# A graph layer's edge sums: ring by edge type, bias counts moved ahead, one-hot buffers of four slots, 544 dense chunks in place of 512

## The chip, the cores and the metric

The kernel runs on one core of one Trainium2 chip. The metric is the device time of one execution in microseconds (us). The engines are TensorE (PE, with its weight loads shown apart as PEld), VectorE (DVE), ScalarE (ACT), GpSimd (POOL) and SyncE (SP, which issues plain DMAs).

## The reference, cut to what matters

There are 12500 nodes with 128 features, 200000 edges sorted by their target `dst`, and four edge types with a 128 x 128 weight and a bias each. Targets are drawn as 12500 u^2, so low-numbered nodes have many edges and high-numbered ones few.

```python
h = jnp.maximum(_layernorm(x, axis=-1), 0.0)
xs = h[src]
msgs = zeros
for i in range(4):
    msgs = msgs + jnp.where((edge_types == i)[:, None], xs @ W[i] + b[i], 0.0)
out = x + jax.ops.segment_sum(msgs, dst, num_segments=12500)
```

## The kernel before, in words

**Table.** First, h is computed for all nodes, split into three bf16 parts and written to a table in device memory (htab). The 200000 edges are 1563 chunks of 128. Two methods share them.

**Dense method, first C0 = 512 chunks.** Their edges end in the lowest nodes, which have many edges each. The kernel counts, for every such target, how many edges come from each source and type, and multiplies the counts by the table. `make_slots` first packs the edges into slots of up to 128 edges of one target (or of two neighbouring targets, past node PAIRS = 558). `count` (L928-986) builds for every slot two one-hot matrices on VectorE, o1 (128x128, L943 or L947) and o2 (128x392, L948), makes them up to AHEAD = 8 slots ahead in two pools of 12 buffers, and multiplies them on TensorE (L959); ScalarE writes the counts as bytes (L962). `multiply` (L988-1030) takes a batch of up to VBMAX = 104 targets: for each of the 98 blocks of the table and each of the 3 parts, one matmul with 4 x 104 = 416 columns (L999), 294 per batch; blocks come in as `hs`, four to a buffer (HB = 4). Then four fp32 matmuls with the type weights (L1015) give the result, which is added to `acc`. While one batch is multiplied the next is counted. With C0 = 512 the kernel's own formulas give ND = 1392 targets, 1167 slots, and 14 batches, one of 76 and 13 of 104.

**Gathered method, the other 1051 chunks.** The first 48 take raw rows of x while the table is still being made (`add_up_raw`). For the other 1003, POOL fetches the 128 table rows of a chunk with one indirect DMA (`gather`, L538), ahead of use in a pool of 20 buffers of two chunks. A chunk's targets fall in a window of `win` nodes, 10 at the start and 26 at the end. VectorE makes a one-hot over type and place in the window (L555, 4 x win wide). Groups are of G = 16 chunks, with four short ones (12, 8, 4, 3) at the end, 68 in all. `sum_up` (L563) adds the rows by type and place with three bf16 matmuls a chunk (L572) into a bank `ps` of four chunks, and ScalarE copies it to `sb` (L575). `weigh` (L580) then counts edges by type with four small matmuls on the one-hots (L590), ScalarE casts them (L594), one matmul adds the biases (L597), and four fp32 matmuls with the type weights (L599, each two instructions on the chip) give `py`, 16 x win columns each. VectorE adds each chunk's window into a `ring` of 2048 + 32 nodes, one row of 128 features to a partition (`ring_adds`, L660).

**Leaving.** When no further edge can reach four blocks of 128 nodes (OT = 4), `put_out` sends them: `leave` transposes them (L685), VectorE adds x (L690), SP writes them out (L692), and the ring's stretch is cleared (L707). The dense nodes leave from `acc` in the same way, after the dense work is done.

**Order.** TensorE, VectorE and ScalarE run in the written order of the main loop over groups (from L1268). A group has 8 parts of two chunks. At each part, the loop runs the dense work up to a share set by `pace` (L1038), which spreads the dense columns evenly over the groups and has all of them done at the first part of the last full group; then the bias counts and weights of the previous group (`finish`), that group's ring additions and the next group's one-hots (`side`), evenly over the parts. SP and POOL are ordered by the scheduler of the compiler.

Of the kernel before, what the change touches and what calls it, by code (L numbers as in the profile page):

```python
# [28 lines left out]

# [19 lines left out]
P = 128  # L49
EPS = 1e-5  # L50
UN = 3
G = 16
# [3 lines left out]
C0 = 512  # L56
VBMAX = 104
MANY = 16
HB = 4
AHEAD = 8  # L60
BEHIND = 0.06
RING = 2048
OT = 4
# [3 lines left out]
SOON = (RAW * 16) + HG  # L67

# [4 lines left out]
def kernel(  # L73
# [148 lines left out]
    ring = const.tile([P, RING + WIN], F32, name="ring")  # L222
# [7 lines left out]
    hpool = mid.enter_context(tc.tile_pool(name="rows", bufs=20))  # L230
# [3 lines left out]
    s_ps = mid.enter_context(tc.tile_pool(name="s_ps", bufs=2, space=PSUM))  # L234
    y_ps = mid.enter_context(tc.tile_pool(name="y_ps", bufs=1, space=PSUM))
# [28 lines left out]
    def prep_edges(m0, m1, prep, QB):  # L264
# [15 lines left out]
        pg = x_ps.tile([P, QB, P], F32, name="pt")  # L280
# [12 lines left out]
        pk = x_ps.tile([P, QB, P], F32, name="pt")  # L293
# [178 lines left out]
    banks = [(s_ps, "ps"), (s_ps, "ps"), (y_ps, "py"), (a_ps, "pa")]  # L472
# [87 lines left out]
    finish = []  # L560
    flushing = []

    def sum_up(t0, g, rows, oh, last):  # L563
        win = window_of(C0 + t0)
        K = NT * win
        sb = spool.tile([P, G * KM], F32, name="sb")[:, : G * K].rearrange("p (g t n) -> p g t n", g=G, t=NT)
        for i0 in range(0, g, SG):
            i1 = min(i0 + SG, g)
            ps = s_ps.tile([P, 512], F32, name="ps")[:, : SG * K].rearrange("p (i n) -> p i n", i=SG)
            for i in range(i0, i1):  # L570
                for c in range(3):
                    nc.tensor.matmul(ps[:, i - i0, :], rows(i, c), oh[:, i, :], start=(c == 0), stop=(c == 2))  # L572
                if i % HG and i + 1 < i1:
                    yield (i + 1) / g
            nc.scalar.copy(sb[:, i0:i1].rearrange("p g t n -> p g (t n)"), ps[:, : i1 - i0, :])  # L575
            yield i1 / g

        finish.append(weigh(t0, g, oh, sb, last))

    def weigh(t0, g, oh, sb, last):  # L580
        win = window_of(C0 + t0)

        def bank():
            to = x_ps.tile([P, G * WIN], F32, name="pt") if last else y_ps.tile([P, G * WIN], F32, name="py")
            return to[:, : G * win].rearrange("p (g n) -> p g n", g=G)

        ohv = oh.rearrange("p g (t n) -> p g t n", t=NT)
        pc = bank()
# [6 lines left out]
        yield True  # L595
        py = bank()
        nc.tensor.matmul(py[:, :g, :], b128, cnt[:, :g, :], start=True, stop=False)  # L597
        for t in range(NT):
            nc.tensor.matmul(py[:, :g, :], wsb[:, t, :], sb[:, :g, t, :], start=False, stop=(t == NT - 1))  # L599
        adds.extend(ring_adds(t0, g, lambda i: py[:, i, :], win))  # L600
        yield True


    def add_up_raw(t0, g, rows, marked):
# [20 lines left out]
        sb = spool.tile([P, G * KM], F32, name="sb")[:, : G * K].rearrange("p (g t n) -> p g t n", g=G, t=NT)  # L625
# [19 lines left out]
    def ring_adds(t0, g, of, win):  # L645
        at = []

        def add(i):
# [10 lines left out]
            to = ring[:, bass.ds(at[i], win)]  # L659
            nc.vector.tensor_tensor(to, to, of(i), ALU.add)  # L660
# [16 lines left out]
    def leave(j0, j1, of, c0):  # L677
# [4 lines left out]
        for j in range(j0, j1):  # L682
            r = rows_of(j)
            k = c0 + (j - j0) * P
            nc.tensor.transpose(pt[:r, j - j0, :], of[:, k : k + r], ident)  # L685
# [11 lines left out]

    def put_out(j0, j1, again):

        c0 = j0 * P % RING  # L700
        n = (j1 - j0) * P
        rest = leave(j0, j1, ring, c0) if j0 else lambda: nc.vector.tensor_tensor(acc, acc, ring[:, :n], ALU.add)

        def end():
            rest()
            if again:
                nc.vector.memset(ring[:, c0 : c0 + n], 0.0)  # L707
            if c0 + n == RING:

                nc.vector.tensor_tensor(ring[:, :WIN], ring[:, :WIN], ring[:, RING:], ALU.add)  # L710
                if again:
                    nc.vector.memset(ring[:, RING:], 0.0)

        return end

    flushes = [(0, NDT, 0)]
# [4 lines left out]
    assert NDT * P <= RING - 512  # L721

    def due(jb):
# [11 lines left out]
    goes = [  # L735
        next((i for i in [*range(RAW + 2, FULL), final - 1] if starts[i] + sizes[i] >= c), final)
        for ja, _, c in flushes
    ]
# [4 lines left out]
    def check_chunks():  # L743
# [3 lines left out]
        nc.vector.memset(low, 0.0)  # L747
# [181 lines left out]
    def count(vs, counts):  # L929
# [6 lines left out]
        made = {}  # L936

        def make(k):
            i, s, by, first, last = todo[k]
            o1 = op1.tile([P, P], BF16, name="o1")  # L940
            o2 = op2.tile([P, NB], BF16, name="o2")
            if by == 1.0:
                nc.vector.tensor_scalar(o1, iota_b, loT[:, s : s + 1], None, ALU.is_equal)  # L943
            else:
                if by is None:
                    by = byT[:, (s - PAIRS) // 2 : (s - PAIRS) // 2 + 1]
                nc.vector.tensor_scalar(o1, iota_b, loT[:, s : s + 1], by, ALU.is_equal, ALU.mult)  # L947
            nc.vector.tensor_scalar(o2, iota_n, hkT[:, s : s + 1], None, ALU.is_equal)  # L948
            made[k] = o1, o2

        done = 0
        for k, (i, s, by, first, last) in enumerate(todo):
            while done < min(k + 1 + AHEAD, len(todo)):
                make(done)
                done += 1
            o1, o2 = made.pop(k)
            if first:
                pb = x_ps.tile([P, NB], F32, name="pt")
            nc.tensor.matmul(pb, o1, o2, start=first, stop=last)  # L959
            if last:  # L960

                nc.scalar.activation(  # L962
                    counts[:, :, i * NT : (i + 1) * NT],
                    pb.rearrange("p (b t) -> p b t", t=NT),
                    AF.Copy,
                    accum_out=both[:, i : i + 1],
                )
            yield (k + 1) / len(todo)
        def check_sums():
            n = len(vs) // 2  # L970
            bi = sdp.tile([P, VB // 2], I32, name="bi")
            nc.vector.tensor_copy(bi[:, :n], both[:, :n])
            bb = sdp.tile([P, 2, VB // 2], I32, name="bb")
            nc.vector.tensor_single_scalar(bb[:, 0, :n], bi[:, :n], 255, op=ALU.bitwise_and)
            nc.vector.tensor_single_scalar(bb[:, 1, :n], bi[:, :n], 8, op=ALU.arith_shift_right)
            bf = sdp.tile([P, 2, VB // 2], F32, name="bf")
            nc.vector.tensor_copy(bf[:, :, :n], bb[:, :, :n])
            top = sdp.tile([P, 2], F32, name="top")
            nc.vector.tensor_reduce(top[:, 0:1], bf[:, :, :n], AX.XY, ALU.max)
            nc.vector.tensor_reduce(top[:, 1:2], bf[:, :, :n], AX.XY, ALU.add)  # L980
            nc.vector.tensor_max(most, most, top[:, 0:1])
            nc.vector.tensor_add(held, held, top[:, 1:2])

        tails.append(check_sums)

    tails = []

# [45 lines left out]
    def columns(gi):  # L1033

        K = NT * window_of(C0 + starts[gi])
        return sizes[gi] * (3 * max(64, K) + 5 * K)
# [188 lines left out]
    for g in groups:  # L1225
# [10 lines left out]
    op1 = counting.enter_context(tc.tile_pool(name="op1", bufs=AHEAD + 4))  # L1236
    op2 = counting.enter_context(tc.tile_pool(name="op2", bufs=AHEAD + 4))
    hsp = counting.enter_context(tc.tile_pool(name="hsp", bufs=4))
    raw_sums = outp.tile([P, OT, D], F32, name="xo").rearrange("p j d -> p (j d)")[:, : RAW * G * win_raw]
    nc.scalar.copy(raw_sums, raw_py[:, : RAW * G * win_raw])  # L1240
    raw_adds = [
        ring_adds(m * G, G, lambda i, m=m: raw_sums[:, (m * G + i) * win_raw : (m * G + i + 1) * win_raw], win_raw)
# [8 lines left out]
    ending = []  # L1251
    leaving = []
    soon = []
    rows = gather(RAW * G, G)
    oh, made = one_hots_of(RAW * G, G)
    for m in made:
        m()
    ordered = ExitStack()
    ordered.enter_context(tc.manual_schedule(engines={mybir.EngineType.PE, DVE, mybir.EngineType.Activation}))
    assert min(goes) >= RAW  # L1260
    for gi, (t0, g) in list(enumerate(zip(starts, sizes)))[RAW:]:
# [3 lines left out]
        side = [lambda of=of: ending.append(put_out(*of)) for of in soon]  # L1265
        if gi > RAW and raw_adds:
            side += raw_adds.pop(0)
        soon = list(flushing)  # L1268
        flushing.clear()
        now = rows, oh  # L1270
        if steps:
            side.append(lambda of=steps[0]: next(of, None))
        if gi < final:
            rows = gather(starts[gi + 1], sizes[gi + 1])
        parts = -(-g // HG)
        when = min(2, parts - 1)
        todo = len(side) + G + 1 + (G if finish else 0)
        for j, part in enumerate(sum_up(t0, g, *now, gi >= FULL)):
            late, tails[:] = list(tails), []
            while work and spent < pace(gi, part):  # L1280
# [3 lines left out]
            for f in late:  # L1284
                f()
            if j == 0:
                if finish:
                    next(finish[0])
                if gi < final:
                    oh, made = one_hots_of(starts[gi + 1], sizes[gi + 1])  # L1290
                    side += made
            if j == when:
                if finish:
                    next(finish.pop(0))
# [178 lines left out]
```

## Time and profile before

| | |
|---|---|
| median of 3 runs | 1405.44 us (1405.35 to 1410.56) |
| the profiled execution | 1402.26 us, span 1400.5 us |
| PE busy | 1314.0 us, 94% of the span |
| PEld busy | 809.6 us, 58% |
| DVE busy | 1002.7 us, 72% |
| ACT busy | 628.8 us, 45% |
| POOL busy | 1032.2 us, 74% |
| DMA | 270.27 MB, mean 193 GB/s |
| the chain that ended last | PE 77%, DVE 10%, DMA 6%, issue 3% |

The matmul times on the page are from the start to the modelled end of one matmul; matmuls overlap in the pipeline, so this document uses the **step**, the time from one start to the next in the timeline, as a matmul's cost. VectorE instructions overlap likewise, though less.

### The profile page before, as it was taken

To read this page: it belongs to the slowest core of one execution; us is meant where nothing else is said; L and a number is where in the kernel's file an instruction comes from. 1 tells how busy PE (TensorE), PEld (TensorE's weight loads), DVE (VectorE), ACT (ScalarE), POOL (GpSimd) and SP (SyncE) were. 2 spreads that over 40 slices of the span, in tenths; PEclk is the share of its full clock that TensorE was granted. 3 is DMA by queue.
4 is the path that set the end of the run, shared out by engine and by line. 5 is a ranking of instruction groups with operands and counts; after the bars stand their busy time and mean duration, and the time that the engine had idled before them with its cause. 6 is when DMAs were issued, how large, how long until landed. Compare 5 with 4: busy or idle time off the path is not lost.

```text
span 1400.5 us, 30850 instructions
## 1 busy us (share of the span) xinstructions
PE 1314.0 (94%) x9776; PEld 809.6 (58%) x9776; DVE 1002.7 (72%) x5153; ACT 628.8 (45%) x2043; POOL 1032.2 (74%) x1078
## 2 busy tenths in 40 slices
PE   4869888999999999999999999999999999999974
PEld 1437466565666666666666656666666655556543
DVE  9990999987887678776767767676777667753533
ACT  6795626244263535445353543535344353361111
POOL 7726777777777777777777777777777777777774
PEclk9995899999999999999999999999999999999977
DMA  8643466676667767676767666777677666767752
GB/s 249 220 172 81 115 193 204 182 219 172 202 186 217 213 202 213 204 220 198 212 190 222 199 202 201 207 208 208 187 208 206 193 199 184 207 189 205 215 146 68
DMA packets 143094, 270.27 MB, mean 193 GB/s; under 512 B 26602, under 2 KB 79004, under 8 KB 142925
## 3 DMA queue, kind: packets, MB, share of 16 engines
q1 hardware_dynamic: 93245, 166.45, 39.0%
q0 software_dynamic: 49680, 101.81, 26.8%
q8 instruction: 77, 1.26, 0.4%
q14 instruction: 92, 0.75, 0.2%
HBM read 252.12 MB, written 16.04 MB: 191 GB/s over the span
## 4 chain that ended last, share of the span: by engine, by line
PE 77%; DVE 10%; DMA 6%; issue 3%; POOL 2%; ACT 1%; SPq 0%; DVEq 0%; POOLq 0%; ACTq 0%
PE pa L999 45%; PE pt L959 12%; PE py L599 8%; PE ps L572 6%; DMA hm<-htab,srcT 5%; DVE o L948 2%; POOL hm L538 2%; DVE o L947 1%; PE ps L629 1%; DVE oh L555 1%; DVE ring L660 1%; DMA hm<-in_x_dram 1%; PE pt L685 1%; PE py L590 1%; PE pt L1015 1%
## 5 line engine op out<-in xcount | busy, mean ns | idle before, releaser
L538 POOL DMA_INDIRECT hm<-htab,srcT x1003 | 974.5, 972 | 332.6 <-issue 190.4
L999 PE MATMUL pa<-counts,hs 128*128 128x416 fp8e4 (+1 forms) x4116 | 892.2, 337 | 0.6 <-ACT sd L1009 0.6
L999 PEld LDWEIGHTS <-hs 128*128 128x128 bf16 x4116 | 391.4, 98 | 257.6 <-issue 1.9
L962 ACT ACTIVATE counts<-pt 128x392 uint16<-128x392 f32 x714 | 355.4, 507 | 342.6 <-PE pt L959 326.1
L948 DVE TENSOR_SCALAR o<-iota_n,hkT 128x392 bf16<-128x392 f16 x1167 | 388.1, 333 | 0.0
L959 PE MATMUL pt<-o,o 128*128 128x392 bf16 x1167 | 372.6, 334 | 10.1 <-DVE o L948 7.0
L555 DVE TENSOR_SCALAR oh<-iota_b,keyT 128x56 bf16<-128x56 bf16 (+8 forms) x1003 | 173.2, 264 | 185.4 <-PE py L590 182.6
L660 DVE TENSOR_TENSOR ring<-ring,py 128x14 f32 (+7 forms) x976 | 167.8, 172 | 95.5 <-PE py L599 46.2
L575 ACT COPY sb<-ps 128x224 f32<-128x224 f32 (+8 forms) x251 | 100.3, 400 | 295.4 <-PE ps L572 278.7
L572 PEld LDWEIGHTS <-hm 128*128 128x128 bf16 x3009 | 162.0, 98 | 101.2 <-DMA hm<-htab,srcT 28.9
L572 PE MATMUL ps<-oh,hm 128*128 128x56 bf16 (+8 forms) x3009 | 186.6, 197 | 23.4 <-DMA hm<-htab,srcT 21.5
L959 PEld LDWEIGHTS <-o 128*128 128x128 bf16 x1167 | 113.0, 98 | 78.9 <-DVE o L948 15.0
L947 DVE TENSOR_SCALAR o<-iota_b,loT,byT 128x128 bf16<-128x128 bf16 x417 | 139.6, 335 | 12.2 <-PE pt L959 10.4
L962 ACT ACTIVATION_READ_ACCUMULATOR counts<-pt 128x1 f32 x714 | 147.1, 206 | 0.0
L599 PE MATMUL py<-sb,wsb 128*128 128x224 f32 (+7 forms) x488 | 130.7, 412 | 0.0
L943 DVE TENSOR_SCALAR o<-iota_b,loT 128x128 bf16<-128x128 bf16 x375 | 98.2, 262 | 13.0 <-PE pt L959 12.7
L599 PEld LDWEIGHTS py<-sb,wsb 128*128 128x128 f32 x488 | 89.3, 196 | 25.3 <-issue 2.9
L947 DVE TENSOR_SCALAR o<-iota_b,loT 128x128 bf16<-128x128 bf16 x375 | 97.1, 259 | 8.2 <-PE pt L959 7.9
L522 POOL DMA_INDIRECT hx<-in_x_dram,srcT x48 | 52.1, 1086 | 19.6 <-issue 9.6
L594 ACT CAST cnt<-py 128x224 bf16<-128x224 f32 (+7 forms) x61 | 24.2, 396 | 56.6 <-PE py L590 56.6
L455 ACT ACTIVATE h<-hm,nmrt,rstdt 128x128 f32<-128x128 f32 x98 | 43.1, 502 | 0.8 <-DVE nmrt L450 0.5
L484 PE MATMUL ps<-h,ident 128*128 128x384 f32 (+1 forms) x34 | 16.7, 575 | 16.1 <-ACT h L455 16.0
(230 smaller groups left out, 601.8 us busy)
## 6 DMA issues: line engine op xcount, KB each, us to landing
hs<-htab SPq DMA_DIRECT2D x336, 384.0 KB
hm<-htab,srcT POOLq DMA_INDIRECT x1003
htab<-h SPq DMA_DIRECT2D x32, 288.0 KB
xo<-in_x_dram SPq DMA_DIRECT2D x23, 256.0 KB
out_dram<-xo SPq DMA_DIRECT2D x23, 256.0 KB
hm<-in_x_dram SPq DMA_DIRECT2D x18, 192.0 KB
hs<-htab SPq DMA_DIRECT2D x14, 192.0 KB
hm<-in_x_dram SPq DMA_DIRECT2D x14, 168.0 KB
```

The source lines that it names most:

```text
L538: one = nc.gpsimd.indirect_dma_start(out=hm[:, (i - h0) * D3 : (i - h0 + 1) * D3], out_offset=None, in_=htab, in_offset=bass.IndirectOffse ...
L555: nc.vector.tensor_scalar(oh[:, i, :], iota_b[:, :K], keyf[:, at : at + 1], None, ALU.is_equal)
L572: nc.tensor.matmul(ps[:, i - i0, :], rows(i, c), oh[:, i, :], start=(c == 0), stop=(c == 2))
L575: nc.scalar.copy(sb[:, i0:i1].rearrange("p g t n -> p g (t n)"), ps[:, : i1 - i0, :])
L599: nc.tensor.matmul(py[:, :g, :], wsb[:, t, :], sb[:, :g, t, :], start=False, stop=(t == NT - 1))
L660: nc.vector.tensor_tensor(to, to, of(i), ALU.add)
L943: nc.vector.tensor_scalar(o1, iota_b, loT[:, s : s + 1], None, ALU.is_equal)
L947: nc.vector.tensor_scalar(o1, iota_b, loT[:, s : s + 1], by, ALU.is_equal, ALU.mult)
L948: nc.vector.tensor_scalar(o2, iota_n, hkT[:, s : s + 1], None, ALU.is_equal)
L959: nc.tensor.matmul(pb, o1, o2, start=first, stop=last)
L962: nc.scalar.activation(counts[:, :, i * NT : (i + 1) * NT], pb.rearrange("p (b t) -> p b t", t=NT), AF.Copy, accum_out=both[:, i : i + 1],)
L999: nc.tensor.matmul(pa[:, : nv * NT], hs[:, j - j0, c * D : (c + 1) * D], counts[:, j, : nv * NT], start=(j == 0 and c == 0), stop=(j == NW ...
```

## The change

It has five parts.

1. **Ring by type, weights late.** The ring gets five rows of windows: the four type sums and the bias sum, over 1024 + 32 nodes instead of 2048 + 32. `sum_up` leaves the type sums in the bank, adds the bias product beside them (one matmul a bank), and VectorE adds 5 x win columns a chunk from the bank into the ring. The copy to `sb`, the four fp32 matmuls of a group and the bank `py` are gone; the freed bank makes `s_ps` three. The type weights come at the flush: `from_ring` does, for each block of 128 nodes, four fp32 matmuls with the ring as the stationary operand and one with the identity for the bias row, in place of one transpose. A flush has two blocks (OT = 2), so there are 44 instead of 24. The first flush starts at block LOWEST = 11, not 0.
2. **Additions late.** A bank's additions run LAG = 2 parts after it was filled, two a part, interleaved with the one-hots.
3. **Bias counts early.** `counts_of` counts the next group's types at the end of the present one, in a bank of `x_ps`.
4. **One-hot buffers of four slots.** o1 and o2 come four slots to a buffer, four buffers each, and are made two to three buffers ahead. `check_sums` is spread over several parts.
5. **C0 = 544.** 32 more chunks are counted and 32 fewer gathered. By the kernel's formulas ND = 1568, 1255 slots, 16 batches (one of 44, 15 of 104), 971 gathers; C0 is no longer a multiple of 128, so `make_slots` has five blocks of chunks instead of four. `hs` is six blocks to a buffer with three buffers (HB = 6), and the pool of gathered rows has 16 buffers.

```diff
-C0 = 512
+C0 = 544
-HB = 4
-AHEAD = 8
+HB = 6
+SLOTS = 4
-RING = 2048
-OT = 4
+RING = 1024
+OT = 2
+LAG = 2
+FLUSH = 3
...
-    ring = const.tile([P, RING + WIN], F32, name="ring")
+    ring = const.tile([P, NT + 1, RING + WIN], F32, name="ring")
...
-    hpool = mid.enter_context(tc.tile_pool(name="rows", bufs=20))
+    hpool = mid.enter_context(tc.tile_pool(name="rows", bufs=16))
...
+    def counts_of(t0, g, oh):
...
+    def sum_up(t0, g, rows, oh, cnt):
+        win = window_of(C0 + t0)
+        many = SG if SG * (NT + 1) * win <= 512 else HG
...
+                    nc.tensor.matmul(
+                        ps[:, i - i0, :NT, :].rearrange("p k n -> p (k n)"),
+                        rows(i, c),
+                        oh[:, i, :],
...
+            nc.tensor.matmul(ps[:, : i1 - i0, NT, :], b128, cnt[:, i0:i1, :], start=True, stop=True)
+            banks.append((ps, i0))
+            adds.append(each[i0:i1])
...
+    def from_ring(j, r, to):
+        c = j * P % RING
+        for t in range(NT):
+            nc.tensor.matmul(to, ring[:, t, c : c + r], wsb[:, t, :], start=(t == 0), stop=False)
+        nc.tensor.matmul(to, ring[:, NT, c : c + r], ident, start=False, stop=True)
...
-                nc.vector.memset(ring[:, c0 : c0 + n], 0.0)
+                nc.vector.memset(ring[:, :, c0 : c0 + n], 0.0)
...
+        sets = []
+        for one in todo:
+            if one[3]:
+                n = sum(t[0] == one[0] for t in todo)
+                if not sets or len(sets[-1]) + n > SLOTS:
+                    sets.append([])
+            sets[-1].append(one)
...
+            lag, many = (LAG, HG) if gi < FULL else (1, SG)
+            some = [ready.pop(0)[1] for _ in range(many) if not flush and ready and ready[0][0] + lag <= at_part]
...
+            if j == max(0, parts - 2) and gi < final:
+                while side:
+                    side.pop(0)()
+                cnt = counts_of(starts[gi + 1], sizes[gi + 1], oh)
```

More of the change, by code (lines that the diff above doesn't have):

```diff
@@ L559 @@
     adds = []
-    finish = []
     flushing = []
-    def sum_up(t0, g, rows, oh, last):
+    def counts_of(t0, g, oh):
         win = window_of(C0 + t0)
[L565 to L585, printed above, removed]
         ohv = oh.rearrange("p g (t n) -> p g t n", t=NT)
-        pc = bank()
+        pc = x_ps.tile([P, G * WIN], F32, name="pt")[:, : G * win].rearrange("p (g n) -> p g n", g=G)
         for t in range(NT):
@@ L701, in put_out, with rest @@
         n = (j1 - j0) * P
-        rest = leave(j0, j1, ring, c0) if j0 else lambda: nc.vector.tensor_tensor(acc, acc, ring[:, :n], ALU.add)
+        if j0 < NDT:
+            assert j0 == LOWEST and j1 == NDT and n <= 512
+            pm = x_ps.tile([P, n], F32, name="pt")
+            for t in range(NT):
+                nc.tensor.matmul(pm, wsb[:, t, :], ring[:, t, c0 : c0 + n], start=(t == 0), stop=(t == NT - 1))
+            def rest():
+                to = acc[:, j0 * P : j1 * P]
+                nc.vector.tensor_tensor(to, to, pm, ALU.add)
+                nc.vector.tensor_tensor(to, to, ring[:, NT, c0 : c0 + n], ALU.add)
+        else:
+            rest = leave(j0, j1, from_ring)
         def end():
@@ L734 @@
     final = len(sizes) - 1
[L735 to L738, printed above, removed]
+    goes = []
+    for ja, _, c in flushes:
+        from_here = goes[-1] + 1 if goes else RAW + 3
+        goes.append(
+            next((i for i in [*range(from_here, FULL), final - 1] if starts[i] + sizes[i] >= c), final)
+        )
     bad = const.tile([P, 5], F32, name="bad")
@@ L1329 @@
                 l()
[L1330 to L1339 removed]
+            for end in before_last:
+                end()
+            while ready:
+                ready.pop(0)[1]()
+            for (ja, jb, _), i in zip(flushes, goes):
+                if i == final:
+                    put_out(ja, jb, False)()
         if gi == FULL - 3:
[L1341 removed]
+            assert q >= BM - 1
             check_chunks()
```

247 lines of the change are left out of this document (142 added, 105 removed).

## The prediction

> **What bounds the kernel now.** I read the busy rows first, then the slices.
>
> ```profile
> PE 1314.0 (94%) x9776; PEld 809.6 (58%) x9776; DVE 1002.7 (72%) x5153; ACT 628.8 (45%) x2043; POOL 1032.2 (74%) x1078
> ...
> PE   4869888999999999999999999999999999999974
> ...
> POOL 7726777777777777777777777777777777777774
> PEclk9995899999999999999999999999999999999977
> ```
>
> PE is full from about 200 to 1340 us at the full clock, and POOL sits at a flat 7. Both need a second look: PE's durations overlap, and POOL's leave out its issue time. The timelines at 600 us show what each really does:
>
> ```profile
> 600.22 1.22 PE L999 MATMUL pa<-counts,hs 128*128 128x416 fp8e4 x6
> 601.27 0.33 PE L959 MATMUL pt<-o,o 128*128 128x392 bf16 x1
> 601.44 0.34 PE L572 MATMUL ps<-oh,hm 128*128 128x64 bf16 x6
> 601.61 0.69 PE L999 MATMUL pa<-counts,hs 128*128 128x416 fp8e4 x3
> ...
> 609.01 1.89 PE L599 MATMUL py<-sb,wsb 128*128 128x256 f32 x8
> 610.74 0.34 PE L572 MATMUL ps<-oh,hm 128*128 128x64 bf16 x6
> ```
> ```profile
> 602.41 0.95 POOL L538 DMA_INDIRECT hm<-htab,srcT  x1 [0.30 <-PE pa L999]
> 603.66 0.95 POOL L538 DMA_INDIRECT hm<-htab,srcT  x1 [0.30 <-issue]
> 604.91 0.95 POOL L538 DMA_INDIRECT hm<-htab,srcT  x1 [0.30 <-issue]
> ```
>
> From one start to the next, six L999 take 1.05 us: a step of 175 ns. Over the trace the median steps are 176 ns for L999 at 416 columns, 129 at 304, 166 for L959, 26 to 43 for L572, 216 for one of the two instructions of an fp32 matmul at 256 columns. Adding up all PE steps from 200 to 1320 us, each form at its median, gives 1077 of 1118 us, and 13 of the other 41 are the type counts L590, whose four matmuls start together and show their cost in one gap. So **PE issues matmuls back to back**; under 30 us in this stretch are waits, some 10 of them for gathered rows. POOL starts a gather every 1.25 us (0.95 busy, 0.30 issue), 80 per 100 us, from 134 to 1385 us: it is at its ceiling too. The two are balanced: whatever adds to PE is paid in full; taking from POOL alone frees little before the tail.
>
> [...]
>
> **The change, part by part.** PE first, over the whole run, in us. Counts after the change follow from the kernel's own formulas at C0 = 544.
>
> - Dense multiply: before 13 x 294 x 0.176 + 294 x 0.129 = 710.6. After, 15 batches of 104 and one of 44 (176 columns; from the forms 129 at 304 and 176 at 416, 0.42 ns a column, so 0.076): 776.2 + 22.3 = 798.5. **+88**.
> - Slots: 1255 - 1167 = 88 x 0.166: **+15**.
> - Type weights of the groups (L599): 520 instructions at their median steps, gone: **-124**.
> - Flush: 85 blocks, each 5 fp32 matmuls of 128 columns = 10 instructions. No such row exists. Nearest: L1015, fp32 weights, 104 columns, 8 in 0.87 us in the timeline at 334 us (111 ns); above, L599 at 160 columns, 136 ns. I take 0.110, nearer 104 columns and where a weight load seems to set the step: 85 x 1.10 = 93.5, and the first flush (8 at 0.216) 1.7: **+95**; with the upper row +117.
> - The 84 ring transposes (L685, 0.109) go, two of acc come: **-9**. Fewer gathered chunks at slightly different windows (L572): -2. Two more L1015 groups: +2. Bias product in four pieces a group with the same columns: +1.
>
> Sum on PE: **+66**. That removing 124 us of weights wins only 38 net of flushes and transposes is plain from columns: before, 16 x win per chunk, after, 20 per node, and there are nearly as many nodes as window columns.
>
> What lies beside PE:
>
> - ScalarE loses the copies (L575, 100 us) and gains 88 count writes of about 0.6 us. It waits on PE (326 us behind L959), so both are hidden, worth 0.
> - VectorE. The ring addition grows from win to 5 x win columns.
>
> ```profile
> L660 DVE TENSOR_TENSOR ring<-ring,py 128x18 f32 x128 | 22.1, 173 | 9.9 <-PE py L599 3.4 <-DVE o L948 2.6 <-DVE ring L660 0.6
> L660 DVE TENSOR_TENSOR ring<-ring,py 128x10 f32 x48 | 7.9, 164 | 1.3
> L690 DVE TENSOR_TENSOR xo<-pt,xo 128x512 f32<-128x512 f32 x23 | 15.7, 684 | 2.9 <-PE pt L685 2.9
> L707 DVE MEMSET ring<- 128x512 f32 x20 | 9.7, 485 | 1.1
> ```
>
> About 1.0 to 1.1 ns a column, so 90 columns take some 250 ns, a step of about 0.28 instead of 0.205: 923 x 0.075 = +69. Clears of 1280 columns about 1.1 us (the row above, 485 for 512; 1232 for 1408 in the tile's forms), 41 of them against 22: +36. Slots 88 x 0.42 (L948 0.232, L943/L947 0.16 to 0.22): +37. In the steady part that makes 17 us of work per group of 20.7 us, 82%, against 75% before; in batches 2 to 4, with 112 slots each, 92%. It is hidden while it is early enough: about 10 us for late buffers. If the cover fails, see the first rival.
> - POOL: 32 gathers fewer, -40, now hidden behind PE. What PE waited for gathers before 1320 us goes: -8. The scheduler places SP's DMAs; SP waits over 900 us for free hs buffers, so 20 more flush transfers and larger hs loads hide in that.
> - Pools of four slots, six hs blocks, 16 row buffers: same depth within a slot or two (8 to 12 slots ahead, 18 against 16 blocks); 0 either way while PE is full, a few us at the start if not.
> - Bias counts early: VectorE idles 182.6 us before L555 behind L590. It is off the chain (L555 1%), so worth little: 0 to -5, kept at 0.
>
> **Start.** VectorE is full from 20 to 100 us. The fifth block makes 60 instead of 40 selections (steps of 0.26) and 13% wider rows in the rest: +8 (0 to +12). POOL's clear of the ring (1.8 us) becomes about 4.6 us, before the first gather, inside that bound. From 134 to 238 us VectorE paces PE with 38 + 121 slots; now 22 + 112, some 15 us sooner, but PE has 16 us less to multiply there (44 targets, not 76): PE's idle time grows by about 6.
>
> **Tail.** One row of the busy times by stretch (length, then PE, PEld, DVE, ACT, POOL with their counts, clock, DMA):
>
> ```profile
> 1337.00:1401.00 64.00, 36.55 (x236) 25.14 (x236) 22.59 (x114) 7.74 (x18) 36.54 (x39) 0.72 0.40 109
> ```
>
> The dense work ends at 1337 us; then 64 us with 39 gathers of 1.25 us, which PE waits for. After the change POOL has some 100 us of slack and runs up to 32 chunks ahead, so 10 or so gathers remain, 14 us. VectorE then sets the tail: 41 chunks x (0.28 + 0.16), flushes, x-additions, checks, about 28, and 8 for the last flush and its DMA: 36 instead of 64, of which PE works about 10 less. Idle: **-19** (-28 to 0).
>
> **Sum** against the profiled execution (1402.3, span 1400.5): PE +66; idle +8 start, +6 slots phase, -8 gathers, +10 VectorE, -19 tail = -3. That gives 1465, and the median of the runs shown lies 3 above that execution: **1468 us**, 4.5% slower. With the upper flush row +22, without tail gain +19, with the best of all idle terms about -25: 1443 to 1498.
>
> **Rivals.**
>
> 1. VectorE becomes a second bound. A bank is free only when its additions have run, and there are three banks for additions two parts late. If one bank a group comes late by one pair of additions (2 x 0.28) at PE, 59 groups give +33: 1501. For: 82 to 92% load on an engine in written order. Against: at 93% (46.6 of 50 us, 250 to 300 us) PE stays full in the trace of before. Chance 0.15.
> 2. The other side: POOL was the pacemaker and PE's fullness is elastic. Then 32 x 1.251 = 40 less, +8 start: 1373. It decides if PE's steps contain 100 us of slack, which POOL's unbroken 1.25 us rhythm allows and PE's steps at their medians don't. 0.05.
> 3. Weight loads don't overlap. The flush's stationary operand changes at every instruction; if its load (L685's PEld row, 150 ns) stood ahead of each of 850 matmuls: +128, 1596. Against it, L685 and L1015 step at 109 to 111 with loads of 150 to 192 shown beside. 0.02. [...]
> 4. Waits give it all back: PE's steps leave 104 us of idle in the whole run; if that fell by 66, no change, 1405. It would need a start and tail that nearly vanish. 0.03.
>
> Forecast 0.75. A measurement here can tell about 0.5% from no change. Slower by over that 0.92, within 0.03, faster 0.05. The range 1438 to 1510 takes in the forecast's own and most of rival 1.
>
> **What would show it.** L999 about 4704 times, 795 us of steps; the new flush line with some 850 fp32 instructions at 105 to 120 ns; PE steps still filling 96% of the middle; gathers no longer every 1.25 us but in bursts, POOL waiting for buffers; dense end near 1428 us and under 45 us of tail. I am wrong if L999's step falls below 170, if PE shows gaps behind L660's successor or o2 (rival 1), or if flush steps exceed 150 (rival 3).

## The result and the profile after

The changed kernel takes **1491.7 us** (median of 4 runs, 1491.0 to 1491.9) where the kernel before takes 1406.3 (4 runs, 1405.4 to 1410.6): a ratio of 1.0608 (interval 1.059 to 1.0626). The forecast was 1468, the range 1438 to 1510. The profiled execution took 1491.6 us, its span is 1489.8.

From the page of the changed kernel, the busy row and the slices of TensorE and GpSimd:

```profile
PE 1395.7 (94%) x10845; PEld 870.8 (58%) x10845; DVE 1096.0 (74%) x5400; ACT 602.7 (40%) x1967; POOL 1015.2 (68%) x1046
...
PE   4989889999999999999999999999999999999876
...
POOL 7626757667777767777777777676777777777660
PEclk9986999999999999999999999999999999999987
```

TensorE is as full as before for 100 us longer. GpSimd is busy for less and no longer flat: its gathers end a slice (37 us) ahead of the end, where before they went on into the last one.

The groups of TensorE and VectorE with their shapes (busy time, mean ns, idle time before):

```profile
L1044 PE MATMUL pa<-counts,hs 128*128 128x416 fp8e4 x4410 | 963.2, 339 | 0.6 <-ACT sd L1054 0.6
L704 PE MATMUL pt<-wsb,ring 128*128 128x128 f32 x672 | 93.6, 285 | 4.5 <-DVE ring L662 4.5
L705 PE MATMUL pt<-ident,ring 128*128 128x128 f32 x168 | 33.7, 284 | 0.0
...
L728 DVE MEMSET ring<- 128x1280 f32 x40 | 45.0, 1125 | 8.7 <-DVE xo L690 8.4 <-DVE acc L720 0.3
L662 DVE TENSOR_TENSOR ring<-ring,ps 128x100 f32 x144 | 36.0, 250 | 2.0 <-issue 1.1
```

The multiply is now L1044 (4410 + 294 instructions), the flush L704 and L705, the ring addition L662, the ring's clearing L728. Steps, from one start to the next, are 176 ns for L1044 (one lasts 339 ns in the rows above, so they overlap), 166 for the slots (L996) and 112 for both flush lines. With every form at its median step, the whole run's TensorE work is **1281.2 us before and 1349.3 after: +68.1**. What lies between the steps went from 108.5 to 127.3 us (+18.9), and the first instruction comes 2.7 us later. Together 89.7, and the spans differ by 89.4.

Two parts of the +68.1 cancel by chance. In the stage that makes the table, the median itself holds waits: one bf16 matmul of 384 columns (L485 before, L487 after) has a median of 614 ns before and 256 after, while its shortest steps are 162 in both, and that alone counts as -11.5 us. The matmuls of `make_slots`, with five blocks of chunks instead of four, add 10.9 us. Without the table's rows, `make_slots` and the first matmul (whose one step is a wait), the sum grew by 69.0.

Where the time between the steps lies, cut at 134 us, at 250 us and at the last dense matmul (1336.3 before, 1437.2 after):

| stretch | before | after | difference | predicted |
|---|---|---|---|---|
| first instruction, and to 134 us | 4.1 + 14.4 | 6.8 + 16.0 | +4.3 | +8 |
| 134 to 250 us (slots first) | 31.2 | 27.8 | -3.4 | +6 |
| 250 us to the end of the dense work | 31.4 | 62.7 | **+31.3** | -8 + 10 |
| behind the dense work | 31.5 | 20.9 | **-10.6** | -19 |

The waits over the whole run say what the third row is made of (us in total, times, longest):

```profile
DVE xo L690 <- PE pt L705: 234.5, 41, 11.2
...
POOL hm L540 <- PE ps L592: 67.3, 63, 10.4
...
PE ps L592 <- DVE ring L662: 36.8, 28, 10.6
```

None of the three stood so in the kernel before. VectorE now stands 234 us in front of the flushes' outputs; GpSimd waits for row buffers; and TensorE waits for **ring additions**, once for 10.6 us. Most of the third row stands there: in the middle stretch 22 gaps of over 0.3 us stand before an L592, 24.7 us in all, that end within 0.1 us of the end of a ring addition. In the kernel before there is no such gap. (The 10.6 us are not among them.) The timeline around one of the 22, VectorE first, then TensorE:

```profile
540.27 0.42 DVE L690 TENSOR_TENSOR xo<-pt,xo 128x256 f32<-128x256 f32 x1 [11.17 <-PE pt L705]
540.91 1.12 DVE L728 MEMSET ring<- 128x1280 f32 x1 [0.21 <-DVE xo L690]
542.07 0.23 DVE L662 TENSOR_TENSOR ring<-ring,ps 128x70 f32 x1
...
547.38 0.22 DVE L662 TENSOR_TENSOR ring<-ring,ps 128x70 f32 x1
```
```profile
546.00 0.33 PE L996 MATMUL pt<-o,o 128*128 128x392 bf16 x1
547.65 0.32 PE L592 MATMUL ps<-oh,hm 128*128 128x56 bf16 x6 [1.32 <-DVE ring L662]
```

VectorE stands 11.2 us in front of the addition of x, then clears, then works off additions and some two dozen one-hots in written order; the addition at 547.38 frees the bank that TensorE wants, 1.3 us late.

The longest stand, the 10.6 us, has another origin, which the prediction did not count at all. Towards the end of the gathers (group FULL - 3), `check_chunks` runs through the flushes with two small VectorE instructions for each:

```profile
1397.41 1.22 DVE L662 TENSOR_TENSOR ring<-ring,ps 128x120 f32 x4
1398.56 0.16 DVE L773 TENSOR_SCALAR step<-rowf 128x8 f32<-128x8 f32 x1
1398.58 0.07 DVE L770 MEMSET low<- 128x8 f32 x1
1398.75 0.17 DVE L776 TENSOR_TENSOR low<-low,step 128x8 f32<-128x8 f32 x1
1398.95 0.29 DVE L773 TENSOR_SCALAR step<-rowf 128x8 f32<-128x8 f32 x1
1399.28 0.17 DVE L776 TENSOR_TENSOR low<-low,step 128x8 f32<-128x8 f32 x1
```
```profile
1406.46 1.75 PE L1044 MATMUL pa<-counts,hs 128*128 128x416 fp8e4 x9
1418.76 0.48 PE L592 MATMUL ps<-oh,hm 128*128 128x96 bf16 x4 [10.55 <-DVE ring L662]
```

With 44 flushes in place of 24, this block, each instruction 0.20 us behind the one it reads from, lasts from 1398.6 to 1417.0. No ring addition runs in that time, the banks stay full, and TensorE stands from 1408 to 1418.8.

### The profile page after: what moved, and what is told of

The parts are those of the page before. It is cut to its first block, busy times and chain, and to the rows that moved or that the text cites. A ratio compares the mean times of both kernels' runs of the same rounds, so it can differ in the third digit from the quotient of the medians.

```text
span 1489.8 us, 33021 instructions
## 1 busy us (share of the span) xinstructions
PE 1395.7 (94%) x10845; PEld 870.8 (58%) x10845; DVE 1096.0 (74%) x5400; ACT 602.7 (40%) x1967; POOL 1015.2 (68%) x1046
## 4 chain that ended last, share of the span: by engine, by line
PE 75%; DVE 18%; issue 2%; ACT 2%; DMA 1%; DVEq 1%; SPq 0%; ACTq 0%
PE pa L1044 44%; PE pt L996 11%; PE ps L592 6%; PE pt L704 5%; DVE o L971 4%; DVE o L977 3%; DVE ring L662 2%; DVE oh L557 2%; PE pt L705 1%; DVE o L973 1%; DVE ring L728 1%; PE ps L631 1%; DVEq L653 1%; PE pt L874 1%; DMA hm<-in_x_dram 1%
## 5 line engine op out<-in xcount | busy, mean ns | idle before, releaser
L1044 PE MATMUL pa<-counts,hs 128*128 128x416 fp8e4 (+1 forms) x4704 | 1001.1, 333 | 0.6 <-ACT sd L1054 0.6
L999 ACT ACTIVATE counts<-pt 128x392 uint16<-128x392 f32 x802 | 398.0, 500 | 629.1 <-PE pt L996 593.8
L1044 PEld LDWEIGHTS <-hs 128*128 128x128 bf16 x4704 | 445.7, 98 | 294.4 <-issue 2.9
L971 DVE TENSOR_SCALAR o<-iota_n,hkT 128x392 bf16<-128x392 f16 x1255 | 409.0, 326 | 12.9 <-PE pt L996 12.7
L996 PE MATMUL pt<-o,o 128*128 128x392 bf16 x1255 | 405.0, 331 | 14.2 <-DVE o L977 3.9
L662 DVE TENSOR_TENSOR ring<-ring,ps 128x70 f32 (+8 forms) x971 | 235.0, 242 | 25.5 <-PE ps L601 8.2
L557 DVE TENSOR_SCALAR oh<-iota_b,keyT 128x56 bf16<-128x56 bf16 (+8 forms) x971 | 223.3, 254 | 39.8 <-PE ps L601 20.0
L592 PEld LDWEIGHTS <-hm 128*128 128x128 bf16 x2913 | 155.4, 99 | 109.7 <-issue 52.4
L592 PE MATMUL ps<-oh,hm 128*128 128x56 bf16 (+8 forms) x2913 | 177.9, 198 | 38.5 <-DVE ring L662 36.8
L690 DVE TENSOR_TENSOR xo<-pt,xo 128x256 f32<-128x256 f32 (+2 forms) x51 | 20.8, 412 | 234.5 <-PE pt L705 234.5
L996 PEld LDWEIGHTS <-o 128*128 128x128 bf16 x1255 | 121.7, 98 | 101.0 <-DVE o L977 18.3
L704 PE MATMUL pt<-wsb,ring 128*128 128x128 f32 x680 | 94.6, 284 | 4.5 <-DVE ring L662 4.5
L704 PEld LDWEIGHTS pt<-wsb,ring 128*128 128x128 f32 x680 | 89.4, 200 | 7.8 <-DVE ring L662 5.0
L728 DVE MEMSET ring<- 128x1280 f32 (+1 forms) x41 | 45.6, 1112 | 8.8 <-DVE xo L690 8.4
L601 PE MATMUL ps<-cnt,b 128*128 128x56 bf16 (+8 forms) x250 | 49.3, 197 | 0.0
```

The costliest lines, as they stand in the source:

```text
L557: nc.vector.tensor_scalar(oh[:, i, :], iota_b[:, :K], keyf[:, at : at + 1], None, ALU.is_equal)
L592: nc.tensor.matmul(ps[:, i - i0, :NT, :].rearrange("p k n -> p (k n)"), rows(i, c), oh[:, i, :], start=(c == 0), stop=(c == 2),)
L662: nc.vector.tensor_tensor(into, into, of(i), ALU.add)
L704: nc.tensor.matmul(to, ring[:, t, c : c + r], wsb[:, t, :], start=(t == 0), stop=False)
L728: nc.vector.memset(ring[:, :, c0 : c0 + n], 0.0)
L971: nc.vector.tensor_scalar(o2[:, k], iota_n, hkT[:, s : s + 1], None, ALU.is_equal)
```

## The experiments

All runs but the last group are on chips on which the kernel before takes 1405 us.

**The flush by itself: flush_bias_only.**

```diff
-        for t in range(NT):
-            nc.tensor.matmul(to, ring[:, t, c : c + r], wsb[:, t, :], start=(t == 0), stop=False)
-        nc.tensor.matmul(to, ring[:, NT, c : c + r], ident, start=False, stop=True)
+        nc.tensor.matmul(to, ring[:, NT, c : c + r], ident, start=True, stop=True)
```

> The changed kernel, its flush with the bias matmul alone: the four matmuls with the type weights of each block are left out, so the gathered nodes get only their biases. Theory (a flush is paid in full on TensorE): 672 instructions of 112 ns are 75 us less, 1415 to 1420. Rival (VectorE's additions and waits set the pace): under 45 us less, above 1447.

Measured: 1414.8 us (ratio 1.0063, 1.0045 to 1.0081), 77 less than the changed kernel. TensorE's steps fell by 75.5 (1349.3 to 1273.8), the time between them by 1. So the flush's steps are paid in full, within the noise: TensorE's sum is the right ledger for this kernel. The 25 us of gaps behind ring additions are not part of that: with a flush a fifth as long they are still 23 gaps and 26.8 us.

**The comparison spread: low_spread.** The two instructions of a flush (L773, L776) are issued one pair a part from group 20 on, ahead of the block.

```diff
-        for (ja, jb, _), i in zip(flushes, goes):   # in check_chunks
+    def find_low():                                 # a generator, one pair at each next()
...
+            if gi >= 20:
+                next(lows, None)
```

> The changed kernel with the 88 small VectorE operations that add up the lowest nodes of the flushes given out two a part from group 20 on, in place of one block of 18 us at group FULL - 3. Theory (the block keeps the ring additions from freeing a bank, and TensorE stands 10.6 us for it): 1479 to 1483. Rival (the dense work runs on meanwhile and the stand is only moved): 1489 to 1493.

Measured: 1479.1 us (ratio 1.0528, 1.0508 to 1.0548), 12.6 less. In its waits the 10.6 us are gone, and the other bank waits are not (25.3 us in the middle, 24.7 in the changed kernel):

```profile
PE ps L592 <- DVE ring L662: 26.5, 28, 2.7
```

So the block cost 12.6 us, and the 25 us of bank waits in the middle are a second, separate one.

**Gathers alone: before_fewer_gathers.** The kernel before, with 31 gathers left out: every second full group reads one pair of chunks' rows from the first of the two, so the sums of those chunks are not the reference's.

> The kernel before with 31 of its 1003 gathers left out (every second group, one chunk uses its neighbour's rows); TensorE does the same work. Theory (both engines are at their limit, TensorE sets the time until the dense work ends): only the waits for rows and part of the tail go, 1380 to 1398. Rival (GpSimd's gathers set the time): 31 x 1.25 = 39 us less, about 1367.

Measured: 1377.2 us (0.9795, 0.9775 to 0.9815), 28 less: a little under the theory's range, though not the rival's 1367. The trace shows both limits: the dense work ends only 3.5 us sooner (1332.8, before 1336.3), which TensorE sets; the tail behind it takes 42.6 us in place of 64.1, which the gathers set. In the kernel before, then, the middle belonged to TensorE and the end to GpSimd.

**The part with 544 chunks: c512.** The changed kernel with 512.

```diff
-C0 = 544
+C0 = 512
```

> The changed kernel with C0 = 512 alone. Theory (TensorE's columns set the time): 14 batches instead of 16 take 88 us of L1044 steps away, 88 slots 15 us, so TensorE would need about 1390 us; 1003 gathers at 1.25 us from 110 us on put the end at about 1400 at the earliest, so 1392 to 1406, with the gathers at 1.25 us again and about the time of the kernel before. Rival (the ring by type and its flushes are what costs, not the 32 chunks): it stays above 1450.

Measured: 1417.5 us (1.0087, 1.0069 to 1.0105), so of the 85 us some 74 come with the 32 chunks; but neither theory's number held. TensorE's steps are 1251.0, 30 below the kernel before, as the columns say; the time between them grew by 43 (108.5 to 151.8), and the kernel is no faster. Dense work ends at 1364.7, gathers at 1394.8 in place of 1385.1: the gathers, 1003 again, set the end and are themselves late; TensorE, with room now, stands more often (38 gaps behind ring additions in the middle, 42.5 us).

**Why the gathers are late: c512_spread_rows20.** First idea: 16 row buffers in place of 20.

```diff
-HB = 6
+HB = 4
...
-    hpool = mid.enter_context(tc.tile_pool(name="rows", bufs=16))
+    hpool = mid.enter_context(tc.tile_pool(name="rows", bufs=20))
```

(with 512 chunks and the spread comparison; the dense loads are cut to make room.)

> A candidate to beat both kernels: the changed kernel with 512 dense chunks as before, the comparison of the lowest steps spread over the parts, 20 row buffers and dense loads of 4 chunks in 3 buffers. Theory: with 512 chunks TensorE's steps are 30 us fewer than before (1251 against 1281) and the gathers set the pace; 16 row buffers cost some 14 us of them (14 gaps of over 2 us, against none before), the comparison some 10 of TensorE: 1417.5 - 12 - 10 = 1393 to 1401 where the kernel before takes 1405, so a ratio of 0.991 to 0.997. Rival: 3 buffers of dense loads are too few and TensorE waits for them, or the gathers are late for another reason: 1408 to 1418. Should the chip be one on which the gathers themselves take some 1550 ns each (the kernel before near 1700), the comparison with 1405 falls away, and only the ratio to before says something: under 1 by the theory.

Measured: 1414.3 us (1.0062, 1.0045 to 1.0079). The theory fell: with 20 buffers the last gather still ends at 1394.6. The dense work ends 12.7 us sooner than in c512 (1352.0) and the kernel only 3 us sooner, so here the gathers do set the end. No gather waits; 18 gathers **take** over 1.5 us each. One of them, GpSimd and then VectorE:

```profile
1157.62 0.95 POOL L540 DMA_INDIRECT hm<-htab,srcT  x1 [0.30 <-issue]
1158.88 2.30 POOL L540 DMA_INDIRECT hm<-htab,srcT  x1 [0.30 <-issue]
1161.48 0.94 POOL L540 DMA_INDIRECT hm<-htab,srcT  x1 [0.30 <-issue]
```
```profile
1158.42 0.42 DVE L690 TENSOR_TENSOR xo<-pt,xo 128x256 f32<-128x256 f32 x1 [4.77 <-PE pt L705]
1159.06 1.12 DVE L728 MEMSET ring<- 128x1280 f32 x1 [0.21 <-DVE xo L690]
```

All 18 have the new wide clearing of the ring beside them, and each ends 0.92 to 0.99 us after that fill does. Gathers with a fill beside them take 1.23 us on average (66 of them), the others 0.96: 66 x 0.27 = 18 us in all. As the others are a little shorter than in the kernel before, all gathers together take 8 us more (982.6 against 974.5), and they start 2.5 us later: that is about the 9.5 us by which they end later. In the kernel before, the fill is 512 columns (0.49 us), and the 22 gathers beside one take 0.97, as do the others. That fits a fill that holds GpSimd up, which is the author's reading; c512_clears below tests it. In the changed kernel (15 such gathers) GpSimd stands 67 us behind L592 besides, so by estimate it costs little there.

**Seven runs on two other chips.** These fell on chips on which the kernel before takes 1703 and 1700 us, so their ratios answer none of the numbers expected; the traces answer some. There, GpSimd pauses for another 1.1 us after every few gathers (the column in brackets is the idle time before the instruction, the trace's own guess at what ended it behind it; the rows are from old_onehots_2):

```profile
549.27 0.95 POOL L540 DMA_INDIRECT hm<-htab,srcT  x1 [0.30 <-issue]
550.52 0.95 POOL L540 DMA_INDIRECT hm<-htab,srcT  x1 [0.30 <-issue]
552.84 0.97 POOL L540 DMA_INDIRECT hm<-htab,srcT  x1 [1.38 <-PE pt L982]
554.11 0.95 POOL L540 DMA_INDIRECT hm<-htab,srcT  x1 [0.30 <-issue]
555.36 0.95 POOL L540 DMA_INDIRECT hm<-htab,srcT  x1 [0.30 <-issue]
556.61 0.95 POOL L540 DMA_INDIRECT hm<-htab,srcT  x1 [0.30 <-issue]
558.99 0.99 POOL L540 DMA_INDIRECT hm<-htab,srcT  x1 [1.43 <-PE pt L982]
```

Some 185 to 210 such pauses (of over 0.8 us) between 134 and 1340 us make the mean interval 1.54 to 1.58 us in every kernel run there, where the kernel before has 1.28 on the first chips. What makes them was not found.

*c512_rows20* (512 chunks, 20 buffers, the comparison in one block):

> The changed kernel with 512 dense chunks and 20 row buffers for the gathers (16 as changed, 20 before), with HB cut from 6 to 4 to make room in SBUF. Theory: with 512 chunks the gathers set the pace; in the run with 512 chunks and 16 buffers they came every 1285 to 1306 ns in most stretches of 100 us against a median of 1251, because a buffer was not yet free, which is 1003 x some 0.04 = 40 us over the span at most, some 10 of it not covered. With 20 buffers they come every 1251 to 1265 and the kernel ends at 1400 to 1409. Rival: the gathers wait because VectorE and TensorE are late with the rows, whatever the number of buffers: 1414 to 1420, as with 16.

Measured: 1732.4 us against 1703.1 (1.0156, 1.0132 to 1.018). It tells nothing of the buffers.

*flush_first*, the flush ahead of its part's dense work (with the spread comparison):

```diff
+            if flush:
+                ending.append(put_out(*out_now.pop(0), True))
             while work and spent < pace(gi, part):
...
-            if flush:
-                ending.append(put_out(*out_now.pop(0), True))
```

> The changed kernel with the comparison of the lowest steps spread over the parts (1479.1 when it was run by itself), and with the flush matmuls of a part issued ahead of the part's dense multiplies instead of behind them. Theory: the waits of VectorE's output addition behind the flush (11.2 us the longest, 234 us in 41 times) make the ring additions late and cost bank waits of some 1.8 us in 100 at TensorE; with the flush first they go: 1462 to 1474. Rival: VectorE has room, the waits cost nothing, and TensorE does the same steps in another order: 1476 to 1482. A second rival: the flush then waits at its own head for the ring's last addition, in TensorE's queue: over 1485.

*adds_bias_only* and, once more, *adds_bias_only_2*: the additions of the type sums are left out, the ring's bias row is still added.

```diff
-            lambda i: banks[i // many][0][:, i - banks[i // many][1]],
-            lambda at: ring[:, :, bass.ds(at, win)],
+            lambda i: banks[i // many][0][:, i - banks[i // many][1], NT, :],
+            lambda at: ring[:, NT, bass.ds(at, win)],
```

> The changed kernel with the lowest steps spread (1479.1 by itself), and with VectorE's ring additions cut to the bias row: the additions of the sums by type are left out, so that each addition is a quarter to a fifth as wide; the matmuls into the banks and out of the ring stay. Theory: the bank handshake with VectorE costs what TensorE's steps do not fill in the middle (some 1.8 us in 100, 20 over the span) and in the tail some 5: 1452 to 1464. Rival: the steps alone set the time and the additions are covered: 1474 to 1481.

> The same kernel as adds_bias_only (the lowest steps spread; VectorE adds only the bias row and leaves out the additions of the sums by type), to be read beside the run of 1479.1 on a chip on which a gather comes every 1250 ns. Theory: VectorE's wide additions hold the banks and the flush, in the middle some 1.8 us in 100 and in the tail some 5: 1452 to 1464. Rival: they are covered, and the steps alone set the time: 1474 to 1481.

Measured: flush_first 1689.8 us (0.9906 of the kernel before, 0.9881 to 0.9931); adds_bias_only 1680.9 (0.9845, 0.9816 to 0.9875) and 1677.2 (0.9883, 0.9819 to 0.9948). In absolute time no theory is tested. The gaps that end behind a ring addition in the middle can be compared between kernels of one chip: 38 of them, 51.7 us, with narrow additions (36, 54.7 in the repeat); 16, 21.2 us, with the flush first; and 36, 60 to 62 us, in old_onehots below, with wide additions and the block. So narrow additions do not clear the waits, and the flush's place has to do with them. VectorE still stands 231 us before L690 in the middle with the flush first; by what way it helps is not shown, nor what it would give on the first chips.

*old_onehots*, and again *old_onehots_2*: one-hots in single buffers, eight slots ahead, as before.

```diff
-SLOTS = 4
+AHEAD = 8
...
-            o1 = op1.tile([P, SLOTS, P], BF16, name="o1")
+            o1 = op1.tile([P, P], BF16, name="o1")
```

> The changed kernel with the one-hot matrices of the slots in single buffers, eight ahead, as before, in place of sets of four. Theory: the one-hots are made well ahead in both forms and the part is worth nothing: 1487 to 1496 against 1491.7. Rival: sets of four free their buffers late and hold up VectorE or TensorE, so the single buffers give 8 us or more: 1484 or less; or they save VectorE semaphore waits, and the old form costs 5 or more: over 1497.

> The same kernel as old_onehots (the one-hot matrices of the slots in single buffers, eight ahead, as before), to be read beside 1491.7 on a chip on which a gather comes every 1250 ns. Theory: worth nothing, 1487 to 1496. Rival: the sets of four hold work up, 1484 or less; or they save waits, over 1497.

Measured: 1701.5 and 1696.2 us, 0.9979 (0.996 to 0.9998) and 0.9986 (0.9957 to 1.0015) of the kernel before. Without a run of the changed kernel there, the part's worth stays open. Still, these two say something else: where a gather comes every 1.55 us, a kernel with 544 chunks, with all that the change adds to TensorE, **costs nothing that these runs resolve** against the kernel before, while the two with 512 chunks (and other buffers) took 1.3 to 1.6% more than the kernel before.

*c512_clears*, the fill of the ring in five short ones:

```diff
-                nc.vector.memset(ring[:, :, c0 : c0 + n], 0.0)
+                for t in range(NT + 1):
+                    nc.vector.memset(ring[:, t, c0 : c0 + n], 0.0)
```

> The run with 512 chunks, the comparison spread and 20 row buffers (1414.3, ratio 1.0062), with the clearing of a flushed stretch of the ring in five fills of 256 columns, one a type, in place of one of 1280 columns. Theory: VectorE's fill of 1280 columns (1.1 us, 40 times) holds up the gather that GpSimd is issuing: in the traces of the three kernels with it, 15 to 18 gathers take over 1.5 us against 0.96, each with such a fill beside it, some 18 us in all, and none of over 1.6 us stands beside the fills of 512 columns in the kernel before, which take 0.5 us. With short fills the long gathers go, the last gather is over near 1384 in place of 1394.6, and the kernel takes 1402 to 1407: a ratio of 0.997 to 1.001. Rival: the long gathers come from something else that happens at a block's end: they stay and it takes 1412 to 1416.

Measured: 1718.1 us against 1699.7 (1.0134, 1.0064 to 1.0205); the expected time can't be read there. The length of the gathers can. Fills of 256 columns take 0.27 us, and **no gather takes over 1.5 us** (the longest 1.31), where c512_rows20, with wide fills under the same pauses, has 8, the other kernels with wide fills on these two chips 3 to 13, and those on the first chips 12 to 18. Beside the short fills some gathers are still longer, by up to 0.28 us, about one fill: 17 take 1.16 to 1.23 us and end 0.92 to 0.99 us after the last of the five fills. One of them, GpSimd and then VectorE:

```profile
562.62 1.22 POOL L540 DMA_INDIRECT hm<-htab,srcT  x1 [0.30 <-issue]
564.14 0.95 POOL L540 DMA_INDIRECT hm<-htab,srcT  x1 [0.30 <-issue]
```
```profile
561.48 1.37 DVE L729 MEMSET ring<- 128x256 f32 x5
```

Whether short fills give the 10 us at the end stays untried on a chip like the first.

Apart from the runs that leave work out, none was faster than the kernel before by more than flush_first's 0.9%, and that on a chip with pauses.

## Why the prediction was right, and where it was off

**The bound.** Right. TensorE's sum decides: predicted +66, measured +68.1, or +69.0 for the rows that the prediction added up. That the two agree within 2 us over the whole run is partly luck, by the two parts that cancel; the prediction had `make_slots` as a cost of VectorE at the start alone. Leaving the flush's weights out returned 77 us for 75.5 of steps.

**Its terms.** Dense multiply: 4704 matmuls, 798.5 us predicted and 798.5 at their median steps. Slots: 1255 at 166 ns, as predicted. Flush: 0.110 us an instruction predicted, 0.112 measured, 97 us with the first flush in place of 95 (some 5 more come from slower steps and waits in the tail). The nearest row, 104 columns of fp32 at 111 ns, was the right one (that a weight load sets this step was the author's guess, and no run shows it: a load takes 192 ns, the step 112); the other end, 0.136, would have been some 20 too many. Two smaller sums don't come out. The outer value of 1498 should be 1468 + 22 + 19 = 1509, which the stated range still covers. VectorE makes 971 of the gathered additions, not 923.

**The third rival** (weight loads that don't overlap) is out. The flush's weight loads show 192 ns from 300 to 1300 us, one ahead of each instruction, and the step is 112.

**The second rival** (GpSimd as pacemaker) is out for these chips: gathers now come in bursts and wait, and the end did not follow them. It had a true core: with 31 gathers fewer the last 64 us of the kernel before became 43, and with 512 chunks and a lighter TensorE the gathers set the end.

**The idle terms failed**: -3 predicted, +21.6 measured. By its own signs the prediction had also called itself wrong if TensorE showed gaps behind the ring additions (rival 1); 22 such gaps came, and the forecast of the tail, under 45 us, was missed. The time still lies in the range because the range took in most of rival 1. With the 2 on TensorE's sum, and without the 3 added for the median (1491.7, and 1491.6 for the profiled execution), that is the 23.7 us by which the forecast was low. Three steps of it:

- "VectorE ... It is hidden while it is early enough: about 10 us for late buffers." Measured 36: 25 of bank waits, which is the mechanism of the first rival at three quarters of its 33 us, and 11 of the block. The step counted VectorE's load (82%) and not its order. VectorE stands 225 us before the flush's outputs in the middle, in 38 stops of up to 11.2 us, and the additions behind in the written order come late by what it then catches up. That is a reading of the timelines; that narrow additions leave the gaps and an earlier flush takes most of them away speaks for it, but both were run on the chips with pauses only, and what the 25 us of gaps are worth in time was not tested. The prediction named the wait that left VectorE (182.6 us behind the type counts) and not the one that came, twice as many flushes, each with matmuls that TensorE has queued behind a part's dense work.
- The **block of small comparisons** doubles with the flushes. It was not in the sum: 12.6 us by low_spread, of which the stand is 11.
- "36 instead of 64" for the tail: 52.7. Gathers end 16 us behind the dense work, as predicted (14). Most of the other 37 us is a chain to and fro between VectorE's additions and the flushes, and the flush, priced at the full clock, runs there at a lower one:

```profile
1440.00:1490.00 50.00, 30.72 (x255) 27.45 (x252) 23.74 (x99) 1.22 (x4) 10.03 (x11) 0.74 0.28 78
...
1471.50:1473.60 2.10, 2.04 (x9) 2.05 (x10) 0.00 (x1) 0.00 (x0) 0.00 (x0) 0.50 0.04 12
1477.80:1479.00 1.20, 1.20 (x16) 1.19 (x15) 0.00 (x0) 0.00 (x0) 0.00 (x0) 1.00 0.00 0
```
```profile
1471.56 2.07 PE pt L704 x8
1473.63 0.43 PE pt L705 x2
1474.06 1.71 PE pt L704 x8
1475.76 0.43 PE pt L705 x2
1476.19 1.43 PE pt L704 x8
1477.61 0.22 PE pt L705 x2
1477.84 0.89 PE pt L704 x8
```

(The first has rows of busy times by stretch, with the granted clock third from the end: 0.74 over the whole stretch, then 0.50 and 1.00. The second is the chain that ended last.) Eight instructions with the type weights take 2.07 us where the clock is 0.50 and 0.89 where it is 1.00. In flush_bias_only the tail is 41.0 us, 11.7 shorter. TensorE's work behind the dense part was 25.4 us where it was 26.0 before, not 10 less.

The start and the slots came out lower than forecast (+4.3 and -3.4, against +8 and +6) and hid 13 us of this.

**Parts at nothing.** ScalarE's work stayed hidden (it waits 594 us behind the slots). For the one-hot buffers the trace gives a hint alone: beyond their steps, TensorE's gaps ahead of slot matmuls are 32 us after the change and 21 before it, most of it from 134 to 250 us (26 and 16), where all gaps together fell by 3.4. How much of that the buffers did is open, and so is what larger dense loads did. Bias counts early were not tried by themselves.

## What to carry to other kernels

When an engine is full, add up its steps: removed and added columns gave that part of the answer within some 3 us here. Keep stages out of the sum whose medians hold waits. Then follow each new result across engines: here VectorE, busy for 74% of the span and working in written order, stood up to 11.2 us for the flushes' outputs, and 24.7 us of gaps at TensorE ended with the ring additions queued behind. Code that runs once per flush grows when flushes become smaller: the block of comparisons cost 12.6 us. A shift of work from one balanced engine to another has a sign only for the rates at hand: 32 chunks moved from gathers to multiplies cost 74 us where a gather comes every 1.28 us; where it comes every 1.55, the kernels with 544 chunks took 1.3 to 1.8% less than those with 512, which differ from them in other buffers too.

## What the runs showed of the hardware that was not expected

**Gathers beside a VectorE fill took longer.** In c512_spread_rows20 a gather that has a fill of 128 x 1280 fp32 (1.125 us) starting between 0.7 us before and 0.2 us after its own start ends 0.92 to 0.99 us after the fill in 20 of 30 cases; the other 10 take their 0.945 as if nothing were there. Beside fills of 256 columns (0.27 us, c512_clears) 17 gathers are longer by up to 0.28 us. Beside fills of 512 columns (0.49 us) in the old ring none of 11 gathers so near to them is longer in the kernel before (0.94 to 0.98 us), so the width alone doesn't decide; why 10 cases escape is open.

**fp32 matmuls of 128 columns stepped at 112 ns** in the changed kernel's flushes where the granted clock was 1.00, one weight load (192 ns) ahead of each, and at 213 ns in the tail (1473.85 to 1475.55 us) where the granted clock was 0.50.

**On two chips GpSimd paused** for 1.1 us more after every four or so gathers (1.38 and 1.43 us idle in place of 0.30 in the rows of old_onehots_2), some 210 to 230 us between 134 and 1340 us, with medians of single instructions unchanged (0.946 us a gather, 176 ns a multiply step).
